# Four source tiles in place of two in each GpSimd sum ahead of TensorE's softmax denominators

## The chip, the cores and the metric

The kernel runs on one core of a Trainium2 chip. A core has five engines that run side by side, each with its own queue of instructions in a fixed order: TensorE (PE, with its weight loads listed as PEld), VectorE (DVE), ScalarE (ACT), GpSimd (POOL) and SyncE (SP), and 16 DMA engines. The metric is the device time of one execution in microseconds; lower is better. It is measured over several runs, and one further execution is recorded by the hardware profiler.

## The reference

Four graph attention layers run one after the other over 3327 nodes with 512 features and one adjacency matrix. Each layer normalises its input, multiplies it by a weight matrix and forms, for every target node, a softmax over its neighbours of a leaky ReLU of a sum of two scores. Layer 2, the one of this case, has a single head and an ELU:

```python
h = jnp.maximum(_layernorm(x, axis=-1), 0.0)
h = features @ W                       # features is the h of the line above
s1 = h @ a1
s2 = h @ a2
e = jax.nn.leaky_relu(s1[:, None] + s2[None, :], negative_slope=ALPHA)
e = jnp.where(adjacency > 0, e, NEG_BIG)
attention = jax.nn.softmax(e, axis=1)
h_prime = attention @ h
return jax.nn.elu(h_prime)             # and x = x + this
```

The heads of the layers are 8, 4, 1 and 8. About one entry in 200 of the adjacency matrix is set, so most nodes have some 10 to 25 neighbours.

## The kernel before

**Lists and dense tiles.** A first stage reads the adjacency matrix, sorts the nodes by the number of their neighbours and keeps a list of neighbours for each. The sorted nodes form `NT` = 26 tiles of 128 rows, tile 0 with the longest lists. In layer 2 the last 17 tiles (25 down to 9) work by lists: `Tile.fetch` lets GpSimd gather the neighbours' rows of 528 numbers from a table in DRAM (L885, one gather for 128 rows of one list position, the tile's own rows coming by a plain DMA on SP), four positions at most to a step. There are 72 such steps. In each, `scored` forms the scores (VectorE, L943; ScalarE, L945), and `group` multiplies and adds the rows into a PSUM bank (VectorE, L969 and L971). The gathers run up to five steps ahead, in five buffers `g`.

**The dense tiles.** The first nine tiles (`ND` = 9) are the class `Wholes`. They take all 26 source tiles, masked by the adjacency matrix, in three passes `p` of three target tiles each (`wide` = 384 target columns), side by side with the steps of the lists. For each source tile `j`, `load` brings the rows `ve` and the mask `mk` (SP), `weights` computes weights `em` of 128x384 (ScalarE, L1192), `masked` applies the mask (VectorE, L1199), and `products` multiplies the weights of each of the three target tiles with the source rows on TensorE (L1220, the weights being the stationary operand; each multiplication shows as two records in the profile), accumulating over `j` in three PSUM banks.

**The denominators.** The softmax's denominator is the sum of a target's weights over all sources. The weights of two source tiles, `2i` and `2i + 1`, share one buffer, and `paired` adds them on GpSimd into `sums` (L1205). Then `added` lets TensorE sum over the 128 partitions: three multiplications with a column of ones, one for each target tile, accumulated over the 13 pairs `i` of a pass into three columns `pd` of a PSUM bank (L1211). After the last source of a pass, `means` takes the reciprocals (VectorE, L1226) and scales the results (ScalarE, L1148), which frees the banks for the next pass.

**The order of the work.** All four compute engines run in the order in which the program is written out. A loop runs over the steps, and `later(s, place, piece)` puts a piece into step `s` at one of three places. A step first issues the gathers of the step five ahead, then does the "first" pieces, then the scores of the next step, the "scored" pieces, its own `group`, and the "last" pieces. `place` spreads the sources of a pass over 19 of its 21 steps. A source of step `s` is masked in `s` ("first"), multiplied in `s + 1`; the pair is added on GpSimd in `s + 1`, and its denominators are taken in `s + 3`. A finished list tile or dense tile is then normalised and projected for the next layer (`Tile.ends`): ScalarE centres it, GpSimd takes the root (L455), TensorE transposes (L475) and projects (L493), and ScalarE writes the new rows (`v`, L500), which SP stores. GpSimd's queue in this layer thus holds gathers, pair sums and roots, in this order within a step.

Of the kernel before, what the change touches and what calls it, by code (L numbers as in the profile page):

```python
# [10 lines left out]
F32 = mybir.dt.float32  # L11
# [4 lines left out]
OP = mybir.AluOpType  # L16
AX = mybir.AxisListType

P = 128
# [827 lines left out]
def tile_gat_lists(ctx: ExitStack, tc: tile.TileContext, x, adj, ws, avs, out, ident, half, slots, L, low, spare, tabx, tabs):  # L847
# [7 lines left out]
    nc = tc.nc  # L855
    NP, F = x.shape
    NT = NP // P
# [15 lines left out]
    wide = 3 * P  # L873
# [5 lines left out]
    one, zero = [spool.tile([P, 1], F32, name=n, bufs=1) for n in ("one", "zero")]  # L879
# [16 lines left out]
    class Tile:  # L896
# [114 lines left out]
        def added(self):  # L1011

            y, xt = self.y, xs[self.t]
            if ELU[self.l]:
                nc.vector.scalar_tensor_tensor(y, self.ex, -1.0, y, OP.add, OP.max)
            if self.W is None:
                nc.vector.tensor_add(xt, xt, y)
                waiting.append((out_v[self.t], self.t, xt))
                return
            total = small.tile([P, 1], F32, name="total")  # L1020
            nc.vector.scalar_tensor_tensor(xt, y, 1.0, xt, OP.mult, OP.add, accum_out=total)
            self.nm = small.tile([P, 1], F32, name="nm")
            nc.vector.tensor_scalar(self.nm, total, -1.0 / F, None, OP.mult)
# [33 lines left out]
        def ends(self, s):  # L1057

            b = s + 1 if ELU[self.l] else s
            cut, project, rows = (0, 1, 2) if HEADS[self.l] == 1 else (2, 3, 6)  # L1060
            e = b + 2
            while any(e <= b1 and a1 <= e + cut for a1, b1 in turning) or \
                    any(e + project < b1 and a1 < e + rows for a1, b1 in projecting):
                e += 1
            if self.W is not None:
                turning.append((e, e + cut))
                projecting.append((e + project, e + rows))
            for d, place, piece in [(s + 1, "scored", self.bent), (b, "last", self.added),
                                    (b + 1, "scored", self.centre), (b + 1, "last", self.root),
                                    (e, "first", self.turn), (e + cut, "last", self.cut),  # L1070
                                    (e + project, "last", self.project), (e + rows, "scored", self.rows),
                                    (e + rows + 1, "last", scatter)]:
                later(d, place, piece)
# [76 lines left out]
    class Wholes:  # L1150
# [50 lines left out]
        def paired(self, p, i):  # L1201

            two = self.pairs.pop((p, i))
            self.sums[p, i] = pools["e"].tile([P, wide], F32, name="sums", bufs=3)
            nc.gpsimd.tensor_tensor(self.sums[p, i], two[:, 0, :], two[:, 1, :], OP.add)  # L1205

        def added(self, p, i):

            both = self.sums.pop((p, i))
            for q in range(3):  # L1210
                nc.tensor.matmul(self.pd[p][:, q:q + 1], both[:, q * P:(q + 1) * P], one, start=(i == 0 and q == 0),  # L1211
                                 stop=(i == NT // 2 - 1), skip_group_check=True)

        def products(self, p, j):
# [17 lines left out]
        def place(self, n):  # L1232

            per = n // (ND // 3)
            for p in range(ND // 3):
                s0 = p * per
                later(s0 - 4 if p else -1, "first", lambda p=p: self.targets(p))
                for j in range(NT):
                    s = s0 + j * (per - 2) // NT
                    later(max(s - 4, -1), "first", lambda p=p, j=j: self.load(p, j))  # L1240

                    if (p, j) == (0, 0):
                        later(-1, "scored", lambda: self.weights(0, 0))
                    later(s, "first", lambda p=p, j=j: (self.masked(p, j), self.weights(*divmod(p * NT + j + 1, NT))))
                    later(s + 1, "first", lambda p=p, j=j: self.products(p, j))
                    if j % 2:
                        i = j // 2
                        later(s + 1, "first", lambda p=p, i=i: self.paired(p, i))
                        later(s + 3, "first", lambda p=p, i=i: self.added(p, i))
                later(s + 3, "last", lambda p=p: self.means(p))  # L1250
                for q in range(3):
                    self.tiles[3 * p + q].ends(s + 3 + q)
# [149 lines left out]
    def later(s, place, piece):  # L1402
        at.setdefault((s, place), []).append(piece)
# [8 lines left out]
    for l in range(NL):  # L1412
# [3 lines left out]
        with ExitStack() as c2:  # L1416
            def pool(name, bufs, **kw):
                return c2.enter_context(tc.tile_pool(name=f"{name}{l}", bufs=bufs, **kw))
# [4 lines left out]
            pools = {"o": pool("ps_o", 1 if whole else 2, **psum)}  # L1423
# [40 lines left out]
            for s in range(-1, at_end):  # L1464
# [10 lines left out]
                if 0 <= s < len(steps):  # L1475
                    tl, i = steps[s]
# [65 lines left out]
```

## Time and profile before

| | |
|---|---|
| median of 3 runs | 2391.89 us (2387.97 to 2394.44) |
| profiled execution | 2390.73 us, of which 2388.9 us are the span from its first to its last instruction |
| mean granted TensorE clock | 0.952 |
| busy, share of the span | PE 87%, DVE 78%, POOL 73%, ACT 40% |
| dense tiles of layer 2 | from about 1482 to 1832 us of the span |
| pair sums on GpSimd, L1205 | 39, 1008 ns each (mean) |
| denominators on TensorE, L1211 | 234 records of 128x1, 246 ns each (mean) |
| gathers on GpSimd in that stretch | 218, about 1.0 us each |

The profile names an instruction by its line, its engine, its operation and the names of the tiles that it writes and reads, and gives for each the time it took, the time its engine sat idle before it, and the instruction whose end ended that idle time (the releaser). "issue" stands for idle time that no recorded event explains. The chain of waits follows the work that ended last back to what released it. Pass 0, 1 and 2 below are the three passes over the source tiles; their last sums end at 1593, 1712 and 1829 us.

### The profile page before, as it was taken

The numbers are of one execution on the slowest core, as the hardware profiler recorded it, in microseconds if no ns is written. First come the engines' busy times: TensorE is split into PE (matmuls) and PEld (weight loads), VectorE is DVE, ScalarE is ACT, GpSimd is POOL, SyncE is SP. The second block draws the span as 40 slices with busy tenths as digits, with TensorE's granted clock in tenths as the row PEclk, the third lists the DMA queues.
The fourth block names the chain that finished last, engine by engine and source line by source line (L and its number), as shares of the span: only waits on it lengthen the run. The fifth ranks groups of instructions, "written<-read, shape, count | busy, mean of one in ns | idle before, by whom it ended". The sixth has DMA issues, their size and how long they took to land.

```text
span 2388.9 us, 27522 instructions
## 1 busy us (share of the span) xinstructions
PE 2069.5 (87%) x7330; PEld 1201.4 (50%) x7330; DVE 1855.8 (78%) x4841; ACT 945.2 (40%) x2532; POOL 1734.1 (73%) x1705
## 2 busy tenths in 40 slices
PE   5777799898898875889999987899898699999997
PEld 4665244454444432545455444456465456556653
DVE  5999788777777745888888884887878488888886
ACT  6996033333331112433333322454444444444430
POOL 9995477777777776666677772878778467777775
PEclk9998899999999997999999998999998899999999
DMA  8995589999888788878888884888887578888885
GB/s 313 332 332 168 179 265 280 297 283 293 276 273 235 235 235 238 240 240 240 240 255 258 253 235 143 275 262 279 265 251 235 163 228 253 248 245 248 251 241 176
DMA packets 261116, 594.77 MB, mean 249 GB/s; under 512 B 103827, under 2 KB 121235, under 8 KB 256598
## 3 DMA queue, kind: packets, MB, share of 16 engines
q0 software_dynamic: 124368, 432.13, 60.3%
q1 hardware_dynamic: 132838, 153.98, 19.8%
q10 hardware_dynamic: 3744, 6.82, 0.8%
q8 instruction: 60, 0.98, 0.2%
q14 instruction: 106, 0.87, 0.1%
HBM read 543.13 MB, written 49.65 MB: 248 GB/s over the span
## 4 chain that ended last, share of the span: by engine, by line
DVE 28%; DMA 19%; POOL 16%; PE 14%; issue 13%; ACT 9%; DVEq 0%; SPq 0%; POOLq 0%; ACTq 0%
DVE m L978 13%; POOL g L885 9%; DMA g<-tab,idxb 8%; POOL key L736 5%; DMA g<-tabx,twiceb 5%; PE whole L1220 4%; PE pv L493 3%; PE bank L983 3%; ACT r L1327 2%; DMA g<-tab,idxa 2%; DVE room L1343 2%; DVE bank L971 2%; DVE z L949 2%; ACT pw L950 1%; PE pi L836 1%
## 5 line engine op out<-in xcount | busy, mean ns | idle before, releaser
L983 PE MATMUL bank<-m,ident 128*128 128x512 f32 x2414 | 1132.4, 616 | 137.5 <-DVE m L978 137.2
L885 POOL DMA_INDIRECT g<-tab,idxb x712 | 682.8, 959 | 235.3 <-issue 163.9
L978 DVE TENSOR_TENSOR m<-g,pw 128x512 f32<-128x512 f32 x1207 | 751.5, 681 | 98.3 <-ACT pw L950 96.4
L983 PEld LDWEIGHTS bank<-m,ident 128*128 128x128 f32 x2414 | 451.5, 196 | 681.4 <-issue 321.4
L950 ACT ACTIVATE pw<-z 128x32 f32<-128x32 f32 (+4 forms) x356 | 68.2, 192 | 984.5 <-DVE z L949 984.3
L493 PE MATMUL pv<-w,hT 128*128 128x264 f32 x1664 | 419.4, 408 | 44.2 <-ACT hT L482 40.6
L885 POOL DMA_INDIRECT g<-tab,idxa x297 | 287.0, 966 | 164.7 <-issue 107.5
L493 PEld LDWEIGHTS pv<-w,hT 128*128 128x128 f32 x1664 | 332.5, 202 | 140.5 <-ACT hT L482 48.3
L885 POOL DMA_INDIRECT g<-tabx,twiceb x342 | 324.3, 948 | 106.4 <-issue 78.7
L1220 PE MATMUL whole<-ve,em 128*128 128x512 f32 x468 | 217.9, 612 | 15.2 <-DVE em L1199 10.0
L736 POOL TENSOR_TENSOR key<-a,keys 128x3328 int32<-128x3328 int32 (+1 forms) x29 | 189.2, 6558 | 4.0 <-DMA a<-in_adj 4.0
L971 DVE SCALAR_TENSOR_TENSOR bank<-g,L,bank 128x512 f32<-128x512 f32 x243 | 183.2, 754 | 6.8
L947 DVE TENSOR_TENSOR z<-g,pw 128x32 f32<-128x32 f32 (+4 forms) x356 | 62.0, 174 | 157.5 <-DMA g<-tabx,twiceb 67.3
L1361 PEld LDWEIGHTS whole<-L,room 128*128 128x128 f32 x1248 | 147.5, 190 | 24.9 <-issue 18.9
L885 POOL DMA_INDIRECT g<-tabx,twicea x99 | 94.6, 955 | 73.7 <-issue 36.8
L1361 PE MATMUL whole<-L,room 128*128 128x130 f32 x1248 | 147.8, 274 | 0.0
L766 DVE MAX8 cand<-key 128x8 f32<-128x208 int32 x416 | 144.0, 364 | 0.1
L1220 PEld LDWEIGHTS whole<-ve,em 128*128 128x128 f32 x468 | 88.0, 195 | 108.1 <-issue 87.0
L1327 ACT ACTIVATE r<-low,L 128x384 f32<-128x384 f32 x208 | 121.2, 583 | 5.1
L475 PE MATMUL pt<-ident,xn 128*128 128x128 f32 x416 | 65.3, 281 | 30.5 <-ACT xn L511 14.9
L475 PEld LDWEIGHTS pt<-ident,xn 128*128 128x128 f32 x416 | 52.2, 149 | 59.7 <-issue 36.9
L978 DVE TENSOR_TENSOR bank<-g,pw 128x512 f32<-128x512 f32 x74 | 51.5, 696 | 37.2 <-ACT pw L950 36.4
(184 smaller groups left out, 2168.9 us busy)
## 6 DMA issues: line engine op xcount, KB each, us to landing
a<-in_adj SPq DMA_DIRECT2D x25, 1664.0 KB, 9.2
tab<-v SPq DMA_DIRECT2D x78, 264.0 KB, 4.0
ve<-tab SPq DMA_DIRECT2D x78, 264.0 KB, 4.3
g<-tab SPq DMA_DIRECT2D x65, 264.0 KB, 4.3
tabx<-vx SPq DMA_DIRECT2D x26, 528.0 KB, 5.4
g<-tab,idxb POOLq DMA_INDIRECT x712, 4.0
low<-tab SPq DMA_DIRECT2D x52, 132.0 KB, 3.7
spare<-tab SPq DMA_DIRECT2D x52, 132.0 KB, 3.8
```

The source lines that it names most:

```text
L475: nc.tensor.transpose(pt[:, k, :], xn[:, k * P:(k + 1) * P], ident)
L493: nc.tensor.matmul(pv[:, s, :HF + 8], hT[:, k, :], W.w[:, k, s, :], start=(k == 0), stop=(k == KC - 1))
L736: nc.gpsimd.tensor_tensor(key[:, c:c + quarter], a[:, c:c + quarter], keys[:, c:c + quarter], OP.mult)
L766: nc.vector.max(cand[:, g * 8:(g + 1) * 8], key[:, g * SEG:(g + 1) * SEG])
L885: nc.gpsimd.indirect_dma_start(out=out_, out_offset=None, in_=table, in_offset=bass.IndirectOffsetOnAxis(ap=which, axis=0))
L950: nc.scalar.activation(self.wt[:, k0:k0 + n, :H], z, AF.Exp)
L971: nc.vector.scalar_tensor_tensor(acc, v, w, acc, OP.mult, OP.add)
L978: nc.vector.tensor_tensor(out_.rearrange("p (s h d) -> p s h d", s=2, d=D), v.rearrange("p s (h d) -> p s h d", d=D), wt[:, k0 + q, :H].re ...
L983: nc.tensor.matmul(self.po, ident, m[:, q, :], start=False, stop=(k0 + q == K - 1), skip_group_check=True)
L1220: nc.tensor.matmul(tl.po.rearrange("p (s m) -> p s m", s=2), e[:, q * P:(q + 1) * P], v.rearrange("p (s m) -> p s m", s=2)[:, :, :F // 2], ...
L1327: nc.scalar.activation(self.r[:, h, :], self.a[:, g, :], AF.Relu, bias=-1.0, scale=self.b[:, j, g:g + 1])
L1361: nc.tensor.matmul(dst, e[:, h, q * P:(q + 1) * P], mov, start=False, stop=(j == NT - 1), skip_group_check=True)
```

## The change

GpSimd adds two pairs together. After the sum of an odd pair it adds the sum of the pair before to it, in place, with a second instruction. TensorE's `added` then runs for the odd pairs and for pair 12, which has no partner, and no longer for the other even pairs. The first accumulation of a pass is that of pair 1 instead of pair 0. The pool of `sums` has four buffers in place of three.

```diff
         def paired(self, p, i):
 
             two = self.pairs.pop((p, i))
-            self.sums[p, i] = pools["e"].tile([P, wide], F32, name="sums", bufs=3)
-            nc.gpsimd.tensor_tensor(self.sums[p, i], two[:, 0, :], two[:, 1, :], OP.add)
+            both = self.sums[p, i] = pools["e"].tile([P, wide], F32, name="sums", bufs=4)
+            nc.gpsimd.tensor_tensor(both, two[:, 0, :], two[:, 1, :], OP.add)
+            if i % 2:
+                nc.gpsimd.tensor_tensor(both, both, self.sums.pop((p, i - 1)), OP.add)
 
         def added(self, p, i):
 
             both = self.sums.pop((p, i))
             for q in range(3):
-                nc.tensor.matmul(self.pd[p][:, q:q + 1], both[:, q * P:(q + 1) * P], one, start=(i == 0 and q == 0),
+                nc.tensor.matmul(self.pd[p][:, q:q + 1], both[:, q * P:(q + 1) * P], one, start=(i == 1 and q == 0),
                                  stop=(i == NT // 2 - 1), skip_group_check=True)
...
                     if j % 2:
                         i = j // 2
                         later(s + 1, "first", lambda p=p, i=i: self.paired(p, i))
-                        later(s + 3, "first", lambda p=p, i=i: self.added(p, i))
+                        if i % 2 or i == NT // 2 - 1:
+                            later(s + 3, "first", lambda p=p, i=i: self.added(p, i))
```

## The prediction

> **What bounds the kernel now.** I first looked for the stretch in which the changed lines run (the tile view: L1205 from 1498.3 to 1827.9 us), then took busy time by stretch: the dense stretch as a whole, and its three passes. Columns: length, busy us (instructions) of PE, PEld, DVE, ACT, POOL, granted clock, DMA share, GB/s.
>
> ```profile
> 1482.00:1832.00 350.00, 322.15 (x1118) 191.46 (x1118) 288.16 (x543) 156.20 (x388) 272.20 (x277) 0.96 0.86 264
> ```
> ```profile
> 1482.00:1594.00 112.00, 98.48 (x323) 55.38 (x323) 92.49 (x167) 53.72 (x166) 86.84 (x89) 0.94 0.88 270
> 1594.00:1712.00 118.00, 114.97 (x413) 70.90 (x412) 98.14 (x188) 51.92 (x112) 94.74 (x97) 0.98 0.88 276
> 1712.00:1830.00 118.00, 107.38 (x379) 64.27 (x380) 96.68 (x186) 49.16 (x107) 89.23 (x91) 0.96 0.81 248
> ```
> TensorE looks like the bound (322 of 350 us) and GpSimd (272) like an engine with room. The time lines of the two engines say otherwise. First GpSimd (start, length, what, idle before it and who ended that):
>
> ```profile
> 1692.79 0.95 POOL L885 DMA_INDIRECT g<-tab,idxb  x1 [0.30 <-issue]
> 1693.76 1.01 POOL L1205 TENSOR_TENSOR sums<-em 128x384 f32<-128x384 f32 x1
> 1694.93 0.97 POOL L885 DMA_INDIRECT g<-tab,idxb  x1 [0.16 <-issue]
> ...
> 1721.00 0.95 POOL L885 DMA_INDIRECT g<-tab,idxb  x1 [2.40 <-ACT neg L1007]
> ...
> 1756.24 0.94 POOL L455 TENSOR_TENSOR root<-ve,half 128x1 f32<-128x1 f32 x1 [3.74 <-DVE ve L1037]
> ...
> 1771.52 1.08 POOL L885 DMA_INDIRECT g<-tab,idxb  x1 [3.42 <-DVE bank L971]
> ```
> Every gather is followed by a gap of 0.30 us that nothing fills (0.16 to 0.18 behind an add or a root). With 159 gaps of the first kind and 59 of the second (0.17) that is 58 of the 78 us in which GpSimd is not busy. What is left, read off the time line row by row, is real waiting: 5.5 us in pass 0 (0.5 at 1522, 0.1 at 1541, 0.25 at 1548, 0.8 at 1558, 0.7 at 1563, 1.6 at 1581, 1.55 at 1586), 2.0 in pass 1 (0.75 at 1659, 1.25 at 1705), 9.2 in pass 2 (2.1 at 1721, 3.75 at 1756, 3.1 at 1771, 0.2 at 1785): 16.7 us in all, none of it between 1587 and 1659 nor between 1785 and 1828. So GpSimd is 94% taken (272 + 58 of 350). TensorE and who makes it wait:
>
> ```profile
> 1697.89 0.73 PE L1211 MATMUL pd<-one,sums 128*128 128x1 f32 x6
> 1698.48 2.82 PE L1220 MATMUL whole<-ve,em 128*128 128x512 f32 x6
> ...
> 1712.51 0.83 PE L1211 MATMUL pd<-one,sums 128*128 128x1 f32 x6 [1.92 <-POOL sums L1205]
> ...
> 1828.92 1.44 PE L1211 MATMUL pd<-one,sums 128*128 128x1 f32 x6 [3.98 <-POOL sums L1205]
> ```
> ```profile
> PE pd L1211 <- POOL sums L1205: 17.2, 5, 6.4
> PE whole L1220 <- DVE em L1199: 10.0, 2, 9.2
> PE whole L1220 <- ACT low L1148: 5.2, 1, 5.2
> ```
> TensorE's largest wait in the stretch is for these very sums, and each pass ends with one (1593.03, 1712.51, 1828.92): GpSimd gets to the thirteenth sum of a pass last. The chain of waits agrees: it runs through GpSimd and its gathers at 1473 to 1515, 1581 to 1593, most of 1629 to 1712 and from 1825 to the layer's end, and through TensorE at 1515 to 1578, 1594 to 1628 and 1730 to 1800.
>
> **The change, part by part.**
>
> *Removed on TensorE.* The denominators run for pairs 1, 3, 5, 7, 9, 11 and 12 in place of 13: 6 groups fewer in each pass, 18 in all. A group delays what follows by 0.59 us (1697.89 to 1698.48), so 18 x 0.59 = 10.6 us of TensorE time. It counts only where TensorE sets the pace.
>
> *Added on GpSimd.* 18 more adds of 128x384.
>
> ```profile
> L1205 POOL TENSOR_TENSOR sums<-em 128x384 f32<-128x384 f32 x39 | 39.3, 1008 | 0.8
> L885 POOL DMA_INDIRECT g<-tab,idxb x127 | 126.8, 999 | 40.4 <-issue 29.2 <-DVE bank L971 3.9 <-ACT neg L1007 2.4
> L1015 DVE SCALAR_TENSOR_TENSOR low<-ex,low 128x512 f32<-128x512 f32 x21 | 17.9, 853 | 11.1 <-ACT ex L1009 11.1
> ```
> What stands behind an add starts 0.96 us after the add's start when it is a root (1514.19 to 1515.15) and 1.17 when it is a gather (1693.76 to 1694.93). No add here reads the result of the one before it, so the price lies between these; I take the middle, 1.06, since a dependent add may or may not wait for its input: 18 x 1.06 = 19.1 us, bounds 17.3 and 21.1. The Trainium skill ("GPSIMD Engine Reference", section 4.1, Engine selection) advises against two-input elementwise work on GpSimd, and its section 3.1 gives 2.6 cycles an element at 1.2 GHz: as an estimate from that page, 832 ns an add and 15.0 us for 18, where the row's 1008 ns would make 18.1.
>
> *What is queued behind it.* On GpSimd each new add stands ahead of the next step's gathers (up to four) and a root; VectorE's scores L943 wait for those gathers, ScalarE's rows L500 for the root. On TensorE an odd pair's matmuls now wait for two adds; products, transposes and projections are queued behind them. The sum of an even pair is no longer waited for, so the 6.44 us wait for pair 0 at 1499 goes, but pair 1's sum, done at 1509.3, comes 1.06 later and takes its place: nothing gained there. No DMA is added or moved; SP's queue keeps its order.
>
> *The sum, pass by pass, along GpSimd.* Pass 0: six adds, 6.4 us, less all 5.5 us of waiting, since a late GpSimd finds its buffers free: +0.9 at the last sum. Pass 1: 6.4 less between 0 and 2.0; both waits are roots waiting for VectorE, which itself waits for gathers, so I take half: +5.4. There TensorE never waits between 1594 and 1701, but its slack to the sums (0.9 us at pair 1, 7.8 at 3, 2.4 at 9, 1.7 at 11, none at 12) is smaller than GpSimd's delay late in the pass, so it will stand waiting at pairs 9, 11 and 12. Pass 2 to 1771: two adds (2.1) against 9.0 of waiting, so TensorE's pace decides, and two groups are gone ahead of it (pairs 0 and 2): -1.2. Then pairs 5, 7, 9 and 11: 4.2 less the 0.2 wait: +4.0, which the gathers behind carry to the layer's end. Sum: 0.9 + 5.4 - 1.2 + 4.0 = +9.1 us.
>
> *What I cost at nothing.* VectorE's instructions whose operands all lie in SBUF stretch when they meet an add; the one that accumulates in PSUM does not (ns: shortest/median/longest):
>
> ```profile
> L943 DVE SCALAR_TENSOR_TENSOR z<-g,L x72: 205/221/1709, 1480.5 to 1860.1; 128x4 f32<-128x4 f32 x58, 128x3 f32<-128x3 f32 x5, 128x1 f32<-128x1 f32 x5, 128x2 f32<-128x2 f32 x4
> L971 DVE SCALAR_TENSOR_TENSOR bank<-g,L,bank x243: 741/756/757, 1485.4 to 1865.1; 128x512 f32<-128x512 f32 x122
> ```
> In the stretch the groups' means exceed their medians by (323-221) ns x 53 for L943, (710-612) x 78 for L1199 and (853-683) x 21 for L1015: 16.6 us, 0.43 for each of 39 adds. For 18 more: 0 to 7.7 us. VectorE's 62 us of idle time cover it; without that cover, +7.7. The Trainium skill ("SBUF — State Buffer", Who interferes with whom) has the rule: a VectorE instruction with two SBUF inputs and a GpSimd instruction that reads SBUF lock each other out, for the whole instruction. By that rule each new add could cost VectorE a full add, 18.1 us, against 7.7 by the rows. A TensorE that stood idle for 3.6 us restarts slowly (the group at 1828.92 takes 1.44, that at 1697.89 0.73), which I also leave out: it would come where GpSimd is behind anyway. The fourth sums buffer costs no time.
>
> **The rivals.**
> - *TensorE is the bound, and its relief shows* (faster). For it: 322 of 350 us busy and a third of the chain. All of it: -10.6, 2381.3 us. Against it: it decides only if GpSimd has room for 6.4 us in every pass, and pass 1 shows 2.0 with a GpSimd wait ending the pass.
> - *The adds vanish in GpSimd's waits* (no change). If all 16.7 us count, wherever they lie, 19.1 - 16.7 = +2.4, 2394.3 us. For it: pass 2's waits exceed its adds by 2.8. Against it: those come before 1785 and four adds after 1771; time gained early can't pay later.
> - *Nothing is absorbed* (much slower). If VectorE, late through the stretched instructions and late gathers, releases buffers later as well, the waits stay: +19.1, 2411.0; with the 7.7, 2418.7. For it: the chain passes through VectorE at 1678 to 1695 and 1713 to 1725. Against it: its idle time.
>
> **How the numbers follow.** The profiled execution took 2390.7 us (span 2388.9 and 1.8 around it), 1.2 under the runs' median of 2391.9; the forecast is the median plus 9.1: 2401.0 us, +0.38%. A difference of 0.3%, 7.2 us, is about what a measurement can tell from no change. Chances: as forecast (+5 to +13 us) 0.60, of which 0.10 lie below 7.2; beyond +13, 0.12; vanishing 0.24; faster 0.04. Slower: 0.50 + 0.12 = 0.62; within 0.3%: 0.24 + 0.10 = 0.34; faster 0.04. The range goes from the vanishing adds (2394) to nothing absorbed (2411).
>
> **What would show it.** Right: L1205 has 57 adds of about 1.0 us, L1211 half its records (126 for 234); GpSimd's waits over 0.3 us nearly gone in pass 0; TensorE's idle time for sums grown, with waits at pairs 9 and 11 of pass 1; passes 0, 1 and 2 longer by about 1, 5 and 3 us; the layers before and after unchanged. Wrong: GpSimd still waiting at 1522 to 1586 (buffers come later: more than forecast), or pass 1 no longer than before (its gathers were never the limit: rival 1 or 2), or an add behind an add well off 1.06 us.

## The result and the profile after

The changed kernel takes 2403.13 us (median of 6 runs, 2395.83 to 2406.31); the kernel before takes 2389.22 us in the 6 runs beside it (2385.39 to 2394.44). The ratio is 1.005, with a 95% interval of 1.0039 to 1.006: slower by 9 to 14 us. The forecast was 2401.0, with +9.1 us. (The two medians lie 13.9 us apart; the ratio, worked out from all the runs, makes about 12.)

The profiled execution of the changed kernel took 2401.08 us, its span 2399.0, against 2390.73 and 2388.9 before. First busy time by stretch, with the columns of the prediction: 350 us from the first masked tile on, and then the three passes, which here end at 1591, 1716 and 1835 us.

```profile
1479.00:1829.00 350.00, 312.19 (x1000) 178.42 (x1000) 290.41 (x534) 152.21 (x380) 282.17 (x288) 0.95 0.83 257
```
```profile
1479.00:1591.00 112.00, 94.26 (x282) 50.14 (x282) 92.85 (x166) 52.67 (x165) 92.08 (x94) 0.93 0.85 266
1591.00:1716.00 125.00, 115.34 (x380) 69.21 (x380) 100.05 (x190) 51.82 (x114) 101.84 (x105) 0.95 0.85 263
1716.00:1835.00 119.00, 102.99 (x340) 59.47 (x341) 100.43 (x185) 49.26 (x107) 93.15 (x97) 0.96 0.80 245
```
TensorE fell from 322 to 312 busy us in 350, as the 18 groups that it no longer runs make it fall; GpSimd rose from 272 to 282. The engine that got lighter was not the one that the time hangs on. The groups of instructions by form from 1480 us to the end of the last sum at 1836 (busy us, mean ns, then idle time before them and what ended it):

```profile
L1199 DVE SCALAR_TENSOR_TENSOR em<-em,c,mk 128x384 f32<-128x384 f32 x77 | 63.0, 832 | 14.2 <-ACT em L1192 7.3 <-issue 6.3 <-ACT b L1186 0.5
...
L1205 POOL TENSOR_TENSOR sums<-em 128x384 f32<-128x384 f32 x39 | 39.3, 1007 | 0.8
L1207 POOL TENSOR_TENSOR sums<-sums 128x384 f32<-128x384 f32 x18 | 19.5, 1083 | 1.4
...
L1213 PE MATMUL pd<-one,sums 128*128 128x1 f32 x126 | 18.7, 264 | 30.0 <-POOL sums L1207 16.9 <-POOL sums L1205 13.1
```
L1207 is the new add. L1213 is L1211 of before: its records fell from 234 to 126, and the time that TensorE stands idle for the sums rose from 17.2 us to 30.0. TensorE's time line shows where:

```profile
1685.70 1.44 PE L1213 MATMUL pd<-one,sums 128*128 128x1 f32 x6 [4.34 <-POOL sums L1207]
1687.00 5.47 PE L1222 MATMUL whole<-ve,em 128*128 128x512 f32 x6
...
1716.30 0.83 PE L1213 MATMUL pd<-one,sums 128*128 128x1 f32 x6 [1.91 <-POOL sums L1205]
...
1834.61 1.44 PE L1213 MATMUL pd<-one,sums 128*128 128x1 f32 x6 [7.59 <-POOL sums L1205]
```
At 1685.70 (pair 9 of pass 1) it waits for a second add; at 1716.30 and 1834.61 passes 1 and 2 end, as before, with a wait for the thirteenth sum. In the kernel before, TensorE waited in pass 1 for the last sum alone. GpSimd's time line, a second add with a root behind it:

```profile
1635.82 1.00 POOL L1205 TENSOR_TENSOR sums<-em 128x384 f32<-128x384 f32 x1
1636.90 1.00 POOL L1207 TENSOR_TENSOR sums<-sums 128x384 f32<-128x384 f32 x1
1637.86 0.55 POOL L455 TENSOR_TENSOR root<-ve,half 128x1 f32<-128x1 f32 x1
```
The root starts 2.04 us after the first add, where it started 0.96 after it before.

Where the time went, by events of the two traces (us):

| event | before | after | difference |
|---|---|---|---|
| first product of pass 0 on TensorE | 1482.9 | 1479.7 | -3.2 |
| end of the last sum of pass 0 | 1593.0 | 1591.0 | -1.9 |
| of pass 1 | 1712.5 | 1716.2 | +3.8 |
| of pass 2 | 1828.9 | 1834.6 | +5.7 |
| first matmul of layer 3 (L1442, after: L1445) | 1879.1 | 1885.9 | +6.9 |
| end of the span | 2388.9 | 2399.0 | +10.1 |

Up to the first product the two programs do the same, and so they do in layer 3; the -3.2 us ahead of the stretch and the +3.2 behind it are taken as differences between two executions (the runs of one kernel lie up to 10 us apart). From the first product to layer 3 the changed kernel takes 10.0 us more. That the times differ by 2 to 4 us more than this is not explained by these two recordings.

### The profile page after: what moved, and what is told of

It reads as the page before. It is cut to its first block, busy times and chain, and to the rows that moved or that the text cites. A ratio compares the mean times of both kernels' runs of the same rounds, so it can differ in the third digit from the quotient of the medians.

```text
span 2399.0 us, 27288 instructions
## 1 busy us (share of the span) xinstructions
PE 2068.0 (86%) x7222; PEld 1193.4 (50%) x7222; DVE 1863.0 (78%) x4841; ACT 944.5 (39%) x2532; POOL 1751.4 (73%) x1723
## 4 chain that ended last, share of the span: by engine, by line
DVE 22%; PE 14%; DMA 14%; POOL 11%; issue 11%; ACT 7%; DVEq 0%; SPq 0%; POOLq 0%; ACTq 0%
DVE m L978 10%; POOL g L885 10%; PE bank L983 7%; DMA g<-tab,idxb 6%; DMA g<-tabx,twiceb 4%; PE whole L1222 3%; DMA g<-tab,idxa 2%; ACT r L1330 2%; PE pv L493 2%; PE whole L1364 2%; DVE bank L971 2%; DVE room L1346 2%; ACT pw L950 1%; DVE z L949 1%; DVE z L947 1%
## 5 line engine op out<-in xcount | busy, mean ns | idle before, releaser
L978 DVE TENSOR_TENSOR m<-g,pw 128x512 f32<-128x512 f32 x1207 | 751.8, 681 | 99.5 <-ACT pw L950 98.5
L1222 PE MATMUL whole<-ve,em 128*128 128x512 f32 x468 | 218.3, 616 | 17.2 <-DVE em L1199 12.0
```

The lines of the kernel that those rows point to most:

```text
L978: nc.vector.tensor_tensor(out_.rearrange("p (s h d) -> p s h d", s=2, d=D), v.rearrange("p s (h d) -> p s h d", d=D), wt[:, k0 + q, :H].re ...
L1222: nc.tensor.matmul(tl.po.rearrange("p (s m) -> p s m", s=2), e[:, q * P:(q + 1) * P], v.rearrange("p (s m) -> p s m", s=2)[:, :, :F // 2], ...
```

## The experiments

I compare the runs by their time and, closer, by lengths in the recorded execution: pass 0 from the start of its first sum (L1205) to the end of its last, passes 1 and 2 from last sum to last sum, and the layer from TensorE's first product to the first matmul of layer 3. Where VectorE takes the sums, the first one starts 4.2 us after the first product, where GpSimd's starts about 15 us after it. Pass 0 by the first sum is therefore not comparable there; the layer is.

All but one of the experiments landed on chips on which every execution takes about 2870 us, the kernel before included. There the DMA engines move 187 GB/s in the time from 1000 us to layer 2's dense stretch and 180 behind it, where they move 234 (from 900 us) and 228 in the first profile, and the mean granted clock is 0.875 and not 0.952. In the dense stretch itself it is 260 GB/s against 264, and 0.95 against 0.96. A time's interval is 7 to 11 us to each side on these chips. The kernel before was therefore recorded there as well. Its passes 1 and 2 are those of the first profile within 0.7 us, so the lengths of these two can be read across; the times, and pass 0, can't. One recording is not exact either: two of one kernel differ by up to 5.3 us in pass 1 and 6.4 in pass 2.

| run | time, ratio to before (95% interval) | pass 0 | pass 1 | pass 2 | layer |
|---|---|---|---|---|---|
| before | | 94.7 | 119.5 | 116.4 | 396.2 |
| the change | 1.005 (1.0039 to 1.006) | 96.4 | 125.2 | 118.3 | 406.2 |
| all sums on VectorE, of four | 0.9957 (0.994 to 0.9974) | 91.2 | 120.5 | 109.7 | 385.5 |
| *slower chips:* before | 1.0009 (0.9978 to 1.004) | 100.1 | 119.7 | 117.1 | 405.1 |
| relief alone | 0.9982 (0.9959 to 1.0005) | 99.8 | 123.8 | 115.5 | 410.4 |
| relief alone, again | 0.9965 (0.9927 to 1.0002) | 99.5 | 118.5 | 115.0 | 405.5 |
| adds alone | 0.9984 (0.9951 to 1.0017) | 103.8 | 124.3 | 119.5 | 414.4 |
| adds alone, again | 1.0008 (0.9975 to 1.0041) | 104.0 | 123.7 | 119.8 | 420.4 |
| memset as second add | 0.9956 (0.9923 to 0.999) | 101.8 | 122.2 | 116.8 | 408.8 |
| second add on VectorE | 0.9974 (0.9947 to 1.0001) | 103.1 | 119.5 | 116.4 | 405.5 |
| the same, again | 0.9977 (0.9942 to 1.0012) | 99.7 | 118.4 | 115.7 | 401.8 |
| change in pass 1 alone | 0.9997 (0.9961 to 1.0033) | 102.0 | 124.3 | 118.7 | 413.1 |
| pairs on VectorE | 1.0045 (1.0008 to 1.0082) | 114.1 | 127.5 | 119.3 | 430.1 |
| the same, again | 1.0052 (1.0027 to 1.0077) | 110.1 | 122.4 | 112.9 | 419.8 |

The theory is the prediction's: GpSimd's queue sets the pace, and each pass ends when GpSimd gets to its last sum. The rivals: TensorE's time counts (its relief of 10.6 us shows); VectorE's instructions, stretched by GpSimd's reads, are the cost; TensorE's wait for a later sum is the cost, not the queue.

### The reference on the slower chips

The kernel before, unchanged.

> The kernel before itself, recorded again, as the reference for the passes of the runs that stand beside it. If the account by passes may be read from one chip to another, passes 1 and 2 take 119.5 and 116.4 us again, within 1 us, whatever the rest of the execution takes.

119.7 and 117.1 us, within 0.2 and 0.7 of the first profile. Pass 0 is 5.4 us longer: GpSimd stands idle once for 6.7 us ahead of a gather there.

```profile
L1205 POOL TENSOR_TENSOR sums<-em x39: 1000/1008/1021, 1828.1 to 2164.0; 128x384 f32<-128x384 f32 x39
```
(Shortest, median and longest in ns, then the first and last start.)

### TensorE's half alone

```diff
-                        later(s + 3, "first", lambda p=p, i=i: self.added(p, i))
+                        if i % 2 or i == NT // 2 - 1:
+                            later(s + 3, "first", lambda p=p, i=i: self.added(p, i))
```
(`start` moves to `i == 1`; `paired` stays as before.)

> Only TensorE's half of the change: denominators for pairs 1, 3, 5, 7, 9, 11 and 12, no second add on GpSimd (the even pairs but 12 are left out of the denominators, so this computes a different softmax). If GpSimd's queue sets the pace, 10.6 us of TensorE work go and the time falls by only 0 to 4 us, because each pass still ends with GpSimd's thirteenth sum, which comes no earlier; what there is comes from pass 2, where GpSimd waits for buffers at 1756 and 1771 (-1.2). If TensorE's time is the bound, -8 to -11 us.

> Again only TensorE's half (13 sums on GpSimd, denominators for 7 of them; the even pairs but 12 are left out of the denominators), to be read beside a kernel before of about 2390 us. If GpSimd's queue sets the pace, 0 to -4 us, and each pass still ends with TensorE waiting for the thirteenth sum. If TensorE's time is the bound, -8 to -11 us. The stretch from the first to the last L1205, 329.6 us before: 326 to 330 by the first, 319 to 322 by the second.

The ratios are 0.9982 and 0.9965, or -5 and -10 us. Both intervals hold 1, and the second holds -8 to -11 us too, so the times don't decide between the two expectations. The first recording's pass 1 has 5.7 us of GpSimd waiting for roots (before: 2.0), which no other run of GpSimd sums has; it can't be read. The second has 118.5 and 115.0: 1.2 and 2.1 us less than the same chips' before, and the stretch from the first to the last sum, 333.0 us, is 3.9 us shorter than the 336.9 there (the 326 to 330 expected was counted from the first profile). From the first product to layer 3 nothing is left of it: 405.5 us against 405.1. Removing 10.6 us of TensorE work is worth 3 to 4 us at most in this recording, as the theory has it, and not 8 to 11.

### GpSimd's half alone

```diff
             nc.gpsimd.tensor_tensor(self.sums[p, i], two[:, 0, :], two[:, 1, :], OP.add)
+            if i % 2:
+                more = pools["e"].tile([P, wide], F32, name="more", bufs=1)
+                nc.gpsimd.tensor_tensor(more, self.sums[p, i], two[:, 0, :], OP.add)
```

> Only GpSimd's half: behind each odd pair's sum a further add of 128x384 that reads that sum and writes a tile that nobody reads; TensorE takes all 13 pairs as before. If GpSimd's queue time is the cost, the same loss as the whole change or about 1 us more: +9 to +15 us. If the change's loss were the adds' price less a real relief of TensorE (10.6 us), the adds alone would cost +20 us or more. If the later sum that TensorE waits for is the cost, and not the queue, this run loses less than half: TensorE's sums are ready before the further add, under +6 us.

> Again only GpSimd's half (18 further adds into a tile that nobody reads, all 13 denominators on TensorE), to be read beside a kernel before of about 2390 us. If the time in GpSimd's queue is the cost: +9 to +15 us, the stretch from the first to the last L1205 at 338 to 343 us (338.9 with the whole change). If a relief of 10.6 us on TensorE is hidden in the change's loss: +20 us or more, 348 us or more. If the later sum for TensorE, and not the queue, is the cost: under +6 us, under 334 us.

The rows of the second recording:

```profile
L1205 POOL TENSOR_TENSOR sums<-em x39: 998/1007/1017, 1802.1 to 2148.5; 128x384 f32<-128x384 f32 x39
L1208 POOL TENSOR_TENSOR more<-sums,em x18: 992/1198/1431, 1814.3 to 2137.5; 128x384 f32<-128x384 f32 x18
```
The times, 0.9984 and 1.0008, show no loss: a miss, and the first interval ends at +5 us, below the +9 that I expected at the least. In the recorded executions the loss is there: from the first to the last sum 347.5 us in both, against 336.9 for the kernel before on such chips, +10.6, and from the first product to layer 3 9 and 15 us more. Their first sum starts at 1801 and 1802 us, and at 1828 in the kernel before, although up to there the programs are the same; in these executions that hides the loss. It does not explain the medians: the execution recorded in the second run was the fastest of its ten, 27 us under their median. Why the medians show no loss is open.

Passes 1 and 2 together take 243.8 and 243.5 us, and 243.5 with the whole change. So with the adds in place, TensorE's relief is worth next to nothing in these passes; and a loss through TensorE's wait for the later sum is out, since here nobody waits for the added instruction.

### A second instruction that reads nothing

```diff
-                nc.gpsimd.tensor_tensor(both, both, self.sums.pop((p, i - 1)), OP.add)
+                nc.gpsimd.memset(pools["e"].tile([P, 1096], F32, name="fill", bufs=1), 0.0)
```

> The changed kernel with each second add replaced by a GpSimd memset of 128x1096 numbers, which should take about as long (1 us) but reads nothing, and writes a tile nobody reads (the even pairs but 12 are left out of the denominators). If the time in GpSimd's queue is the cost, +8 to +14 us like the whole change. If the cost is VectorE's instructions that stretch while GpSimd reads, most of it goes: under +5 us, and the mean of L1199, 832 ns in the changed kernel, falls back to about 710.

The groups of this run's GpSimd, and a stretch of its time line:

```profile
L1205 POOL TENSOR_TENSOR sums<-em 128x384 f32<-128x384 f32 x39 | 39.3, 1008 | 0.8
L1207 POOL MEMSET fill<- 128x1096 f32 x18 | 18.4, 1022 | 0.0
```
```profile
1931.69 1.01 POOL L1205 TENSOR_TENSOR sums<-em 128x384 f32<-128x384 f32 x1
1932.62 1.03 POOL L1207 MEMSET fill<- 128x1096 f32 x1
1933.60 0.67 POOL L455 TENSOR_TENSOR root<-ve,half 128x1 f32<-128x1 f32 x1
```
Passes 1 and 2 take 122.2 and 116.8: together 239.0, 2 to 3 us over before instead of 7. From the first to the last sum it is 340.8 us, 3.9 over the kernel before on such chips, and the time, 0.9956, is even below it. By my own limit (under +5) this falls on the rival's side, though the mean of L1199 did not fall back: 781 ns.

But the memset is also the cheaper filler, which the expectation didn't allow for. The root starts 1.91 us after the first add, not 2.04 at the least; the gap from a sum to the gather behind it is 2.13 us here, 2.32 in the changed kernel, 2.41 with the adds alone and 1.17 without a second instruction. GpSimd's time from the first sum to the last can be added up from its rows (us; a wait is idle time beyond the prediction's fixed gaps of 0.30 us ahead of a gather, or 0.17 behind an add or a root; the 39 first sums, 39.3 to 39.4 us, and the fixed gaps, 54.0 to 54.3, are alike in all; a memset starts a little before the add ahead of it ends, which is taken off):

| | before | the change | *slower chips:* before | adds alone | again | memset |
|---|---|---|---|---|---|---|
| first to last sum | 330.6 | 339.9 | 336.9 | 347.5 | 347.5 | 340.8 |
| second instructions, with the idle time ahead of them | | 20.9 | | 22.2 | 22.1 | 17.1 |
| 202 gathers | 203.1 | 203.0 | 205.1 | 202.5 | 201.1 | 202.0 |
| 20 roots | 15.4 | 13.7 | 15.8 | 14.1 | 14.1 | 14.3 |
| waits | 18.4 | 8.9 | 22.2 | 15.3 | 16.9 | 13.9 |

The memset run is 6.7 us shorter than the adds alone, and 5 of these are the lower price. The waits shrink by 8.3 us behind memsets, by 5.3 and 6.9 with the adds alone, where TensorE keeps all its denominators, and by 9.5 with the change. So what could come by way of VectorE is 1.4 to 3.0 us against the adds alone, and nothing against the change. VectorE's instructions of this run and of the second run with the adds alone:

```profile
L1199 DVE SCALAR_TENSOR_TENSOR em<-em,c,mk 128x384 f32<-128x384 f32 x78 | 59.9, 781 | 22.7 <-issue 11.7 <-ACT em L1192 9.8 <-ACT hT L482 1.2
...
L1021 DVE SCALAR_TENSOR_TENSOR x<-low,x 128x512 f32<-128x512 f32 x27 | 18.8, 694 | 0.9
L1015 DVE SCALAR_TENSOR_TENSOR low<-ex,low 128x512 f32<-128x512 f32 x27 | 18.6, 688 | 18.7 <-ACT ex L1009 11.6 <-issue 4.7 <-ACT c L1187 2.4
L943 DVE SCALAR_TENSOR_TENSOR z<-g,L 128x4 f32<-128x4 f32 (+3 forms) x72 | 17.5, 243 | 42.5 <-DMA g<-tab,idxa 22.7 <-issue 11.5 <-DMA g<-tab,idxb 4.2
```
```profile
L1199 DVE SCALAR_TENSOR_TENSOR em<-em,c,mk 128x384 f32<-128x384 f32 x78 | 62.9, 821 | 23.7 <-ACT em L1192 11.5 <-issue 9.7 <-ACT c L1187 2.4
...
L1015 DVE SCALAR_TENSOR_TENSOR low<-ex,low 128x512 f32<-128x512 f32 x27 | 21.8, 806 | 19.8 <-ACT ex L1009 8.5 <-issue 6.3 <-ACT neg L1007 3.2
L1021 DVE SCALAR_TENSOR_TENSOR x<-low,x 128x512 f32<-128x512 f32 x27 | 20.8, 769 | 0.9
L943 DVE SCALAR_TENSOR_TENSOR z<-g,L 128x4 f32<-128x4 f32 (+3 forms) x72 | 20.7, 287 | 36.3 <-DMA g<-tab,idxa 17.1 <-issue 7.5 <-remote 6.4
```
Behind memsets L1015, L1021 and L943 are near their shortest, behind reading adds they are not; L1199 stayed long. Over these four lines the time beyond the shortest usual lengths (counted as under "What I costed at nothing") is 14.8 us here, 13.2 in the kernel before on such chips, and 25.8 and 25.5 in the two runs with the adds alone. So a reading add stretches VectorE's instructions and a memset hardly does. Whether that costs the kernel time is not shown: the queue time explains most of the difference between the fillers, and no run has the one without the other.

### The second add on VectorE

```diff
-            if i % 2:
-                nc.gpsimd.tensor_tensor(both, both, self.sums.pop((p, i - 1)), OP.add)
+        def joined(self, p, i):
+            both = self.sums[p, i]
+            nc.vector.tensor_tensor(both, both, self.sums.pop((p, i - 1)), OP.add)
...
-                        if i % 2 or i == NT // 2 - 1:
+                        if i % 2:
+                            later(s + 3, "first", lambda p=p, i=i: self.joined(p, i))
+                            later(s + 4, "first", lambda p=p, i=i: self.added(p, i))
+                        elif i == NT // 2 - 1:
                             later(s + 3, "first", lambda p=p, i=i: self.added(p, i))
```

> The changed kernel with the second add moved to VectorE, two steps after the pair's first add, and the denominators one step later. GpSimd's queue is as before the change. If GpSimd's queue is the bound, -4 to +2 us: 18 adds of about 0.6 us on VectorE (10.8 us) are covered by its 62 idle us, and TensorE's relief shows as little as in the run with the relief alone. If VectorE's time or its waits for GpSimd's sums decide, +6 us or more.

> Again the second add on VectorE, to be read beside a kernel before of about 2390 us. On the other chip passes 1 and 2 took 119.5 and 116.4 us between their last sums, the same as the kernel before here (119.5 and 116.4). If GpSimd's queue sets the pace and TensorE's relief is worth next to nothing: -4 to +2 us, passes of 119 to 120 and 115 to 117 us. If VectorE's time decides: +6 us or more. If TensorE's relief counts: -8 us or more.

0.9974 and 0.9977, and 119.5 and 116.4, then 118.4 and 115.7 us: the passes of the kernel before, or 1.3 us less in each; from the first product to layer 3, 0.4 us more and 3.3 less. The same arithmetic, with the same relief of TensorE, costs nothing once it is off GpSimd; 18 adds of 0.55 us are lost in VectorE's idle time. (This takes both the queue time and the reads off GpSimd, so it doesn't part the theory from the rival by VectorE.) And TensorE's relief shows as little as in the run with the relief alone.

### The change in pass 1 alone

```diff
-            if i % 2:
+            if p == 1 and i % 2:
...
-                        if i % 2 or i == NT // 2 - 1:
+                        if p != 1 or i % 2 or i == NT // 2 - 1:
```
(`start` is that of pair 1 in pass 1 and of pair 0 in the others.)

> The change in pass 1 alone; passes 0 and 2 as before. From the last sum of pass 0 to the last sum of pass 1 the trace shows 119.5 us before and 125.2 with the whole change. If the pass-by-pass account holds, this run keeps +5 to +6.5 us there, passes 0 and 2 stay as before (93.7 and 116.4 us between their last sums, within 1 us), and the time rises by 4 to 8 us. If the waits of pass 2 absorb what pass 1 lost, the time rises by under 2 us.

Pass 1 takes 124.3 us, 4.6 more than the same chips' before: a little under the 5 to 6.5 expected. Pass 2, where nothing was changed, takes 118.7, 1.6 over that before and outside the 1 us I allowed; its longest wait for a root is 5.0 us, not 3.7. Whether that follows from a late pass 1 or from the chip, one recording doesn't say. What is plain is that pass 2 doesn't give back what pass 1 lost. The time, 0.9997 with 10 us to each side, decides nothing.

### All sums on VectorE

```diff
-            nc.gpsimd.tensor_tensor(both, two[:, 0, :], two[:, 1, :], OP.add)
+            nc.vector.tensor_tensor(both, two[:, 0, :], two[:, 1, :], OP.add)
             if i % 2:
-                nc.gpsimd.tensor_tensor(both, both, self.sums.pop((p, i - 1)), OP.add)
+                nc.vector.tensor_tensor(both, both, self.sums.pop((p, i - 1)), OP.add)
```

> The changed kernel with all 57 adds of the sums on VectorE instead of GpSimd, at the same place in the order. From the first masked tile to the last sum, the stretch took 329.6 us before (first to last L1205 in the trace) and 338.9 with the change. If GpSimd's queue is what the change overloads, taking 57 adds (about 60 us) off it leaves TensorE as the pace: TensorE's 322 us less 10.6, and VectorE's 288 busy us plus 57 x 0.61 less the stretching through GpSimd's reads (16.6), about 306: faster than before by 5 to 20 us, and faster than the changed kernel by 15 to 30. If the sums were not the limit and the loss came from somewhere else (a later start of the denominators, more work on the chain), about the changed kernel's time, +5 us or more over before.

2379.41 us against 2389.95 of the kernel before on the same chip: 0.9957 (0.994 to 0.9974), faster than both kernels. From the first product to layer 3 it takes 385.5 us, against 396.2 before and 406.2 with the change. (From the first to the last sum it would be 321.4 against 330.5, but these sums start 11 us earlier in the pass.) Its groups:

```profile
L1199 DVE SCALAR_TENSOR_TENSOR em<-em,c,mk 128x384 f32<-128x384 f32 x78 | 46.4, 612 | 14.6 <-ACT em L1192 14.6
L1205 DVE TENSOR_TENSOR sums<-em 128x384 f32<-128x384 f32 x39 | 21.4, 549 | 0.0
...
L1213 PE MATMUL pd<-one,sums 128*128 128x1 f32 x126 | 15.2, 236 | 0.0
```
An add that took GpSimd 1.0 us takes VectorE 0.55. TensorE no longer waits for a sum (0.0 idle us before L1213), and L1199 takes 612 ns on average and 659 at most, with no addition on GpSimd beside it. GpSimd's waits over 0.3 us, for roots and buffers, now come to 38.6 us in the three passes, 7.0 with the change. The same with sums of two:

```diff
-            nc.gpsimd.tensor_tensor(self.sums[p, i], two[:, 0, :], two[:, 1, :], OP.add)
+            nc.vector.tensor_tensor(self.sums[p, i], two[:, 0, :], two[:, 1, :], OP.add)
```

> The kernel before with its 39 pair sums on VectorE in place of GpSimd; all 13 denominators of a pass stay on TensorE. With all sums of four on VectorE the time fell by 10.5 us (0.9957). If that came from emptying GpSimd's queue, with TensorE's pace setting the rest, this run keeps the 10.6 us of TensorE work and loses most of the gain: -4 to +2 us. If TensorE's 10.6 us don't matter even then, it is as fast as the sums of four on VectorE: -8 to -12 us.

> Again the 39 pair sums on VectorE, 13 denominators on TensorE. If TensorE's pace sets the rest once GpSimd's queue has room: pass 2 at 111 to 115 us (116.4 before, 109.7 with sums of four on VectorE), the time -4 to +2 us against before. If TensorE's 10.6 us don't matter even then: pass 2 at 109 to 110 us, -8 to -12 us. If the slow passes of the first recording (127.5 and 119.3 us) belong to the kernel and not to its chip, they come again.

This is a miss: slower than before, by 1.0045 and 1.0052, on the slower chips, though GpSimd waits 31 and 26 us in pass 0 alone. In the second recording pass 2 takes 112.9 us, in the 111 to 115 that TensorE's pace allows with all its denominators, so the slow pass 2 of the first (119.3) did not come again. From the first product to layer 3 the two take 25 and 15 us more than the kernel before there. In the second, by the end of TensorE's last denominators of each pass, pass 0 is 1.0 us longer, pass 1 6.4 longer, pass 2 4.1 shorter, and the time from there to layer 3 11.4 longer. So the loss lies in pass 1 and behind the passes; what makes it was not found. Whether the sums of four on VectorE would lose there too is open: the one kernel never ran on a chip of the faster kind, and the other never on the slower ones. The gain of 10.5 us is shown for one chip only, and the reading "GpSimd's queue relieved, so faster" holds for the sums of four, not for the sums of two.

## Why the prediction was right

**The bound.** Right: TensorE lost 10 busy us and the kernel got slower. The relief alone is worth 3 to 4 us at most in the stretch and, with the adds there, next to nothing; the same additions off GpSimd cost nothing. That the cost is the second add on GpSimd is shown by the recordings of the stretch, though not by the times on the slower chips; that it is all queue time, as the prediction has it, is not.

**The price of an add.** Slightly under: 1.06 us was the middle of 0.96 and 1.17. A second add delays a gather by 2.32 - 1.17 = 1.15 us and a root by 1.19 (2.15 less 0.95, without the one that also waits for VectorE), as an average, so the upper end: 20.9 us for 18, not 19.1. It starts 1.08 to 1.10 us after the first, not 0.96, and lasts up to 1.34 us.

**Pass 0.** Forecast +0.9, measured +1.7 (96.4 - 94.7). All of GpSimd's waits over 0.3 us are gone, as forecast; most of the difference, 0.6 us, is the dearer add.

**Pass 1.** Forecast +5.4, measured +5.7. Of its two waits one went (0.75) and one stayed (1.25 at 1709.73), near the half that I took. TensorE waits at pairs 9 and 12, as forecast, and at pair 1 (0.3), but not at pair 11. After the wait at pair 9 it runs slowly: three products (six records) in 5.47 us where they take 2.8. I had left that out; it doesn't lengthen the pass, which ends with GpSimd.

**Pass 2.** Forecast +2.8 (-1.2 + 4.0), measured +1.9. At the gather that waits for its buffer (1771.52 before, 1773.98 after) the changed kernel has gained 1.3 us against the pass's start, as forecast (1.2). The rest of the pass costs 3.2, less than 4.0: its four second adds take 4.4 us, but its 36 gathers and two roots are 1.2 us shorter than before.

**Behind the passes.** Not in my sum: from the last sum to layer 3 another 1.2 us. There TensorE restarts after 7.6 us of idle time instead of 4.0, and its first projections take 6.77 and 6.21 us, against 5.97 and 5.27 before. The passes' errors (+0.8, +0.3, -0.9) and this make +10.5 from the first sum on, for +9.1 forecast.

**Luck.** That the passes add up to +9.4 for +9.1 is partly luck. The adds cost 1.8 us more than forecast and the waits gave back 9.5 us instead of 10.0; against that the 20 roots took 1.7 us less (15.4 to 13.7), which I had not counted on. In the three other runs with a second instruction in every pass they take 14.1 to 14.3 us as well, in those without one on GpSimd 14.9 to 15.8; what shortens them was not looked for.

**What I costed at nothing.** VectorE's instructions did stretch. In the changed kernel's stretch L1199, L943, L1015 and L1021 exceed their shortest usual lengths (614, 221, 683 and 694 ns) by (832-614) x 77 + (298-221) x 54 + (743-683) x 24 + (723-694) x 24 = 23 us, against 17 before: 6 us more, inside my 0 to 7.7. With the adds alone it is 12 us more than before on such chips, above that bound and below the full add of 18.1; with all sums on VectorE the excess is 0.1 us. The time is hidden in VectorE's idle time, as forecast; whether it also delayed roots and buffers that GpSimd waits for is what the memset run left open, at 0 to 3 us. The rule that I cited from the Trainium skill ("SBUF — State Buffer", Who interferes with whom), that only GpSimd's reads get in the way of an instruction with two SBUF inputs, fits L943, L1015 and L1021 behind memsets; L1199, at 781 ns, doesn't show it.

**The rivals.** That TensorE's relief shows and that the waits swallow the adds are out, by the result and the recordings of the runs with each half. Nothing absorbed (+19) is out too: 9.5 of the 18.4 us that GpSimd waited before went.

## What to carry to other kernels

Before work is moved to the engine with the lower busy share, count the fixed gaps in its queue: GpSimd, 272 of 350 us busy, was at 94% with the gaps behind its gathers, and TensorE at 92% was waiting for it at the end of each pass. The engine not to load further is the one whose work others wait for at the end of a stage: 18 adds of 1 us there cost 10 us, and the same 18 on VectorE none. That taking work off it makes a kernel faster doesn't follow: with sums of four on VectorE it did, on one chip, with sums of two it didn't, on others. And an add that costs its own engine 1 us also stretches the instructions of another: VectorE's four lines were 11 to 17 us over their shortest lengths with 39 adds on GpSimd, 23 to 26 with 57, and 0.1 to 0.2 with none.

## What was not expected

- On some chips the unchanged kernel took 2842 to 2913 us instead of 2385 to 2394, with the DMA engines moving 207 GB/s on average and not 249. The steady passes 1 and 2 of layer 2 kept their lengths (119.7 and 117.1 against 119.5 and 116.4), so that a change in them could be read there when the total could not show it. What slows those chips was not looked for.
- A GpSimd add that reads what the instruction before it wrote varies from 993 to 1335 ns (with other second operands, 992 to 1431), while the first adds stay within 997 to 1024 and memsets within 1016 to 1033. Why was not separated.
